# One-pass norms around an early mean, layer 3 two pairs behind layer 2, and the first pair by tiles, in a fused four-layer kernel

## The chip, the cores and the metric

The kernel runs on one core of a Trainium2 chip. The time is that of one execution on the device in microseconds, taken as the median over runs. Five engines work side by side, each on its own queue of instructions in a fixed order: TensorE (PE in the profile, with PEld for its weight loads), VectorE (DVE), ScalarE (ACT), GpSimd (POOL) and SyncE (SP, which issues DMAs here). An engine whose next instruction has to wait holds up everything queued behind it.

## The reference

The input x has the shape (T=4, B=8, 512, 512). Four layers follow one another, each of the form x = x + f(norm(x)). The first is an attention-like block with spiking neurons, the second a 13x13 blur of each channel, the third a quantised 3x3 convolution over the eight channels, the fourth a plain 3x3 convolution over them. In the code these are layer 0 to layer 3.

```python
def _gn(v, G=4, eps=1e-5):                      # group norm
    B_, C_, H_, W_ = v.shape
    g = v.reshape(B_, G, C_ // G, H_, W_)
    m = jnp.mean(g, axis=(2, 3, 4), keepdims=True)
    s = jnp.var(g, axis=(2, 3, 4), keepdims=True)
    return ((g - m) / jnp.sqrt(s + eps)).reshape(v.shape)

x = x + _L0_conv_ref(_gn(x), ...)
x = x + _L1_conv_ref(_gn(x), w1)                # 13x13, each channel alone
# layer 2: sx = 127 / max|v|, sw = 127 / max|w2|, v = _gn(x)
x = x + conv3x3(round(v * sx), round(w2 * sw)) / (sx * sw) + b2
x = x + conv3x3(_gn(x), w3) + b3                # layer 3
```

What matters for the change: `_gn` needs the mean and the variance over two channels of a whole image (index t) before the next layer may use them. Layer 2 needs in addition the largest normed value over all images, for its scale, so it can't start before layer 1 has ended. Layer 3 needs the norm of its own t alone.

## The kernel before

**Layer 1** (class `Layer1`) goes through four groups of two channels, through both channels of each and through the four t. An image is four PSUM tiles of 16 matmuls in the trace. Each tile is evicted by ACT (L850); DVE takes its statistics (`bn_stats`, L852) and its largest and smallest value (`hi` and `lo`, L858) from the evicted tile. `next_norm` makes the mean `m` and the reciprocal deviation `r` of a finished group of channels; for the last group it runs after the last image (the two last `hi` and `lo` reductions of that image are put into its pauses, L905) and nothing of layer 1 is left to lie beside it.

**The norm itself** is `group_steps` (L164 to L198), a generator whose `yield`s let the caller place other work. `bn_stats` leaves a mean and a sum of squared deviations per row and half. A first sum of the means on DVE (`gsum`, L177) goes through a matmul with a constant matrix (`gps`, L180) that adds over the partitions and divides. With the mean back, DVE takes the squared distances of the rows' means, adds the rows' own variances (L189 to L195), sums again, and a second matmul (again L177 and L180) gives the variance. POOL raises it to the power -1/2 (L197).

**Layers 2 and 3** (`layers23`, from L1037) work on windows of rows. Two windows lie on the two halves of the partitions, two such tiles are a pair, and there are 22 pairs in each of the four t, 88 in all; the last pair of a t has half a tile. For a pair of layer 2: SP loads x (L1096), ACT norms it (`y`, L1113), DVE rounds it to `xq` (L1125), POOL copies two outer phase rows of `xq` (L1129 and L1130: a row of pixels is stored as four phases, and a tap to the left of phase 0 is phase 3 moved by one), PE makes three matmuls a tile, one for each dx (L1146), and DVE adds the result to x and writes it into the ring `x3` (L1153). For the statistics of layer 3's norm, rows of t=0 get their sum from this DVE instruction and their squares from ACT (L1160); from t=1 on every second tile does, the others get `bn_stats` on DVE (L1165).

Layer 3 reads the ring. It needs halo rows of neighbouring windows (`halos`; DMAs on SP in the first t, on POOL later, L1304), edge columns (POOL, L1242), and the band of weights scaled with `r` of its own t (`band_t`, L1218). It makes 24 matmuls in the trace per pair (L1249), ACT evicts them (L1258), SP stores them (L1265).

The order is written out in the loop at the end of `layers23`: step n does layer 2 of pair n, then layer 3 of pair n - 22 - `LAG`; `RING` = 23 + `LAG` pairs fit into the ring. `norm3` is started after the last pair of a t and moved on by `next(norm)` twice a step:

```python
        next(norm, None)
        ...
        if n >= N_PAIRS + LAG:
            t, p = divmod(n - N_PAIRS - LAG, N_PAIRS)
            with tc.issue_after(did):
                behind = (layer3(t, p, *norms[t]),)
        if n < n_all and n % N_PAIRS == N_PAIRS - 1:
            norm = norm3(n // N_PAIRS)
        next(norm, None)
```

A scheduler then fixes the order on each engine from this order, moving cheap instructions up where it expects them to be ready; `tc.issue_after` keeps an instruction behind a given one.

Of the kernel before, what the change touches and what calls it, by code (L numbers as in the profile page):

```python
# [35 lines left out]
F32 = mybir.dt.float32  # L36
# [13 lines left out]
G = 4  # L50
# [21 lines left out]
LAG = 3  # L72
# [9 lines left out]
def windows(k):  # L82

    p, j = divmod(k, 2)
    every = [(a, 4 * p + 2 * j + (a ^ j)) for a in range(2)]
    return [(a, q) for a, q in every if q < W_ALL]

# [42 lines left out]
def network(ctx: ExitStack, tc: tile.TileContext, i: dict, out: bass.AP):  # L130
# [68 lines left out]

    def group_stats(*args, **kwargs):  # L200
        steps = group_steps(*args, **kwargs)
        while True:
            try:
                next(steps)
            except StopIteration as end:
                return end.value
# [29 lines left out]
    late = ctx.enter_context(pool("late", side="right"))  # L236
    st2 = late.tile([P, T, B, W1_N // 2 // N_PS1, 6], F32, name="st2")
# [8 lines left out]
    with ExitStack() as s:  # L246
        ps_1 = s.enter_context(pool("ps_2", space=PSUM))
        layer1 = Layer1(
            s, tc, x1d, x2d, avg, group_steps, r1, mr1, st2, m2, r2, most, w_sum, head, ps_1, pool
        )  # L250
        layer1.group(0)
        for g in range(1, G):
            if g == 1:
                with ExitStack() as behind:
                    for op in layer1.started:
                        behind.enter_context(tc.issue_after(op))
                    norm1(G - 1, ps_1)
                    w23 = weights23(tc, i, late, early["y"], ps_1, ident)
            layer1.group(g)
        layer1.next_norm(G - 1)  # L260
    first.close()
    with ExitStack() as s:
        layers23(
            s, tc, x2d, out, ident, ind, mask2, avg_same, group_steps, m2, r2, most, w23, early, pool
        )
# [544 lines left out]
class Layer1:  # L810
    def __init__(
        self, s, tc, x1d, x2d, avg, group_steps, r1, mr1, st2, m2, r2, most, w_sum, head, ps_1, pool
# [3 lines left out]
            nc=nc, x1d=x1d, x2d=x2d, avg=avg, group_steps=group_steps, r1=r1, mr1=mr1, st2=st2, m2=m2,  # L816
# [56 lines left out]
    def group(self, g):  # L873
# [6 lines left out]
        for b in range(g * PAIR, (g + 1) * PAIR):  # L880
# [4 lines left out]
            for t in range(T):  # L885
                self.image(g, b, t, off)
                if g > 0 and b % PAIR == 0 and t == 0:
                    self.next_norm(g - 1)

    def next_norm(self, g):  # L890
# [3 lines left out]
        steps = self.group_steps(  # L894
            self.st2[:, :, g * PAIR : (g + 1) * PAIR].rearrange(
                "p t b k (h z) -> p t (b k h) z", z=3
            ),
            T, PAIR * n_a * 2, None, self.avg, self.ps_1, f"x2_{g}",
        )

        while True:
            try:
                next(steps)
                if g == G - 1 and self.last_ends:
                    nc.vector.tensor_reduce(*self.last_ends.pop(0))  # L905
                next(steps)
            except StopIteration as end:
                m, r = end.value
                break
# [127 lines left out]
def layers23(  # L1037
    s, tc, x2d, out, ident, ind, mask2, avg_same, group_steps, m2, r2, most, w, early, pool
# [81 lines left out]
    def quantise(t, p):  # L1120
# [8 lines left out]
        nc.gpsimd.tensor_copy(xq[:, :, 0, 1:], xq[:, :, PH, : NV - 1])  # L1129
        nc.gpsimd.tensor_copy(xq[:, :, PH + 1, : NV - 1], xq[:, :, 1, 1:])  # L1130
# [6 lines left out]
    def layer2(t, p):  # L1137
# [5 lines left out]
        for j, k in enumerate(ks):  # L1143
            ps = ps_2.tile([P, D], F32, tag="conv2", name="ps_conv2")
            for dx in range(3):
                mm = nc.tensor.matmul(  # L1146
                    ps[:n_p, :], lhsT=w["band2"][:n_p, j, dx, :n_p],
                    rhs=xq[:, j, dx : dx + PH, :], start=dx == 0, stop=dx == 2,
                )
# [43 lines left out]
    def norm3(t):  # L1193
# [3 lines left out]
        ks = by_sums(t)  # L1197
        ks = slice(ks.start, ks.stop, ks.step)
        total, squares = (w["sums"][t % 2][:, j, ks] for j in range(2))
        nc.vector.tensor_scalar_mul(total, total, 1.0 / D)  # L1200
        for h in range(2):
            nc.vector.tensor_copy(st3[:, ks, 3 * h + 1], total)
        nc.vector.tensor_scalar(total, total, w["m"][:, t : t + 1], None, op0=ALU.subtract)
        nc.vector.tensor_mul(total, total, total)
        nc.vector.scalar_tensor_tensor(
            total, total, -1.0 * D, squares, op0=ALU.mult, op1=ALU.add
        )
        for h in range(2):
            nc.vector.tensor_scalar_mul(st3[:, ks, 3 * h + 2], total, 0.5)
        st3 = st3.rearrange("p k (h z) -> p (k h) z", z=3)  # L1210
        nc.vector.tensor_scalar_add(st3[:, :, 1], st3[:, :, 1], w["b2"])
        m, r = yield from group_steps(
            st3.unsqueeze(1), 1, W2_N * 2, mask2, avg_same, ps_1, f"x3_{t}"
# [63 lines left out]
    for n in range(n_all + N_PAIRS + LAG):  # L1277
# [19 lines left out]
        next(norm, None)  # L1297
        if n_chunk < n <= n_all + 3 and n % n_chunk == 3:
            t, p = divmod(n - 3 - n_chunk, N_PAIRS)
            copies = list(halos(t, p, p + n_chunk))  # L1300
            at_once = -(-len(copies) // (n_chunk - 2))
# [3 lines left out]
        if n >= N_PAIRS + LAG:  # L1305
            t, p = divmod(n - N_PAIRS - LAG, N_PAIRS)
            with tc.issue_after(did):
                behind = (layer3(t, p, *norms[t]),)
        if n < n_all and n % N_PAIRS == N_PAIRS - 1:
            norm = norm3(n // N_PAIRS)  # L1310
        next(norm, None)
# [36 lines left out]
```

## Time and profile before

| what | value |
| --- | --- |
| median of 3 runs | 2902.28 us (2898.83 to 2903.59) |
| profiled execution | 2902.63 us, of which the profile's span is 2900.8 us |
| PE busy | 2818.8 us (97%) |
| DVE busy | 2183.1 us (75%) |
| ACT busy | 549.2 us (19%) |
| POOL busy | 868.8 us (30%) |
| last matmul of layer 1 starts | 2482.89 us |
| first matmul of layer 2 starts | 2495.05 us |
| first matmul of layer 3 starts | 2569.18 us |
| last store issued | 2896.87 us |

The times in the profile count from the start of its span. Rows of a timeline give start, length, engine with line, operation, what is written from what, form, and in brackets the idle time of that engine before it with what ended it. Lengths of DVE and PE rows overlap with the next instruction of the same engine: the distance from start to start is what an instruction costs its engine.

### The profile page before, as it was taken

The page shows a single profiled execution, that of the slowest core. Times are in us where ns is not written, and L with a number is a line of the kernel's source. Part 1 is how long each engine was busy: PE and PEld are TensorE (multiplying, and loading weights), DVE is VectorE, ACT ScalarE, POOL GpSimd, SP SyncE. Part 2 cuts the span into 40 slices and gives each one's busy share as a digit, 9 for nine tenths or more (in the row PEclk, how much of TensorE's full clock was granted, in tenths as well). Part 3 has the DMA queues.
Part 4 walks back from the last instruction along what each step waited for, and adds up shares of the span by engine and source line. Part 5 has one row for each costly group of instructions (what it writes and reads, how often), then busy time and mean ns, then how long its engine had stood idle before and what let it go on. Part 6 is the DMA issues. An engine that isn't in the chain of part 4 may idle for free. (4 is left out here: it accounts for less than half of the span.)

```text
span 2900.8 us, 36559 instructions
## 1 busy us (share of the span) xinstructions
PE 2818.8 (97%) x12868; PEld 1302.5 (45%) x12868; DVE 2183.1 (75%) x3888; ACT 549.2 (19%) x851; POOL 868.8 (30%) x1920
## 2 busy tenths in 40 slices
PE   7999999999999999999999999999999999689999
PEld 3444555545555545455555555445333333223334
DVE  6897788788779878878877886886665665888870
ACT  2200100011010001001000000110111121677774
POOL 2242243333234323333422343332311111232220
PEclk9899999999999999999999999999999999999999
DMA  8433222223222232222222122212877788699975
GB/s 209 115 89 76 59 67 67 74 74 74 59 67 67 77 76 68 59 67 67 75 67 51 45 59 52 52 45 75 221 203 207 209 219 224 157 201 234 224 191 148
DMA packets 326127, 324.01 MB, mean 112 GB/s; under 512 B 21519, under 2 KB 240439, under 8 KB 325831
## 3 DMA queue, kind: packets, MB, share of 16 engines
q1 hardware_dynamic: 263024, 239.48, 34.1%
q0 software_dynamic: 19776, 56.14, 6.0%
q10 hardware_dynamic: 43143, 26.05, 3.1%
q8 instruction: 101, 1.65, 0.3%
q14 instruction: 83, 0.68, 0.1%
HBM read 212.44 MB, written 103.65 MB: 109 GB/s over the span
## 5 line engine op out<-in xcount | busy, mean ns | idle before, releaser
L524 PE MATMUL ps_in<-w_v,xn 128*128 128x512 f32 x1024 | 459.1, 599 | 5.4 <-DVE w_v L359 5.4
L524 PE MATMUL ps_in<-w_kq,xn 128*128 128x512 f32 x1024 | 449.8, 592 | 0.0
L843 PE MATMUL ps_conv<-x,bt 112*64 112x512 f32 x2048 | 445.2, 592 | 0.1
L524 PE MATMUL ps_in<-xn,w_kq 128*128 128x512 f32 x1024 | 444.9, 592 | 0.0
L560 PE MATMUL ps_b<-toep,vtok 128*64 128x512 bf16 x3072 | 367.1, 383 | 0.4 <-DVE v_o L575 0.4
L475 ACT ACTIVATE h_q<-v_q,c_half 128x512 f32<-128x512 f32 x96 | 69.1, 721 | 1473.6 <-DVE v_q L471 893.9
L500 POOL TENSOR_TENSOR h_v<-h_v,c_v 128x512 f32<-128x512 f32 x96 | 121.8, 1269 | 728.0 <-DVE h_v L499 700.1
L587 PE MATMUL ps_out<-wp,so 128*128 128x512 f32 x1024 | 308.7, 444 | 0.0
L609 POOL COPY x1s<-x1s 128x2 f32<-128x2 f32 (+1 forms) x1024 | 226.6, 275 | 273.0 <-DVE x1s L598 273.0
L524 PEld LDWEIGHTS ps_in<-xn,w_kq 128*128 128x128 f32 x1024 | 194.3, 190 | 232.5 <-issue 220.4
L524 PEld LDWEIGHTS ps_in<-w_kq,xn 128*128 128x128 f32 x1024 | 194.3, 190 | 220.7 <-issue 206.2
L524 PEld LDWEIGHTS ps_in<-w_v,xn 128*128 128x128 f32 x1024 | 191.4, 191 | 222.9 <-issue 212.1
L843 PEld LDWEIGHTS ps_conv<-x,bt 112*64 112x64 f32 x2048 | 146.5, 135 | 288.0 <-issue 286.0
L560 PEld LDWEIGHTS <-vtok 128*64 128x64 bf16 x3072 | 176.1, 111 | 155.1 <-issue 5.6
L1249 PE MATMUL ps_conv<-x,band_t 64*64 64x512 f32 x2040 | 242.7, 595 | 0.0
L587 PEld LDWEIGHTS ps_out<-wp,so 128*128 128x128 f32 x1024 | 192.6, 188 | 94.0 <-issue 57.8
L1153 DVE SCALAR_TENSOR_TENSOR x<-ps_conv,inv,x 128x512 f32<-128x512 f32 (+1 forms) x172 | 186.1, 1169 | 46.9 <-PE ps_conv L1146 46.7
L598 DVE SCALAR_TENSOR_TENSOR x1s<-v_p,xr 128x256 f32<-128x256 f32 x256 | 187.6, 773 | 14.6 <-DMA x<-x1s 3.8
L865 POOL DMA_DIRECT2D x<-xo x128 | 71.4, 564 | 330.6 <-ACT xo L850 316.3
L850 ACT ACTIVATE xo<-ps_conv,off 128x512 f32<-128x512 f32 x128 | 87.6, 687 | 430.6 <-PE ps_conv L843 307.4
L500 POOL TENSOR_TENSOR h_k<-h_k,c_k 128x512 f32<-128x512 f32 x96 | 122.0, 1270 | 138.4 <-DVE h_k L499 138.4
L1146 PE MATMUL ps_conv<-xq,band 128*128 128x512 bf16 (+1 forms) x516 | 131.5, 391 | 31.3 <-POOL xq L1129 31.3
(193 smaller groups left out, 3113.8 us busy)
## 6 DMA issues: line engine op xcount, KB each, us to landing
x<-x SPq DMA_DIRECT2D x64, 917.0 KB
x<-x SPq DMA_DIRECT2D x168, 256.0 KB
x<-x1s POOLq DMA_DIRECT2D x128, 262.0 KB, 2.7
xq<-in_x SPq DMA_DIRECT2D x128, 256.0 KB
xr<-in_x SPq DMA_DIRECT2D x128, 256.0 KB
out<-o SPq DMA_DIRECT2D x164, 192.0 KB
xs<-in_x SPq DMA_DIRECT2D x112, 256.0 KB
x<-xo ACTq DMA_DIRECT2D x128, 128.0 KB
```

Of the source, the lines that this page charges most:

```text
L500: nc.gpsimd.tensor_add(h, h, c_twice[n])
L524: mm = nc.tensor.matmul(ps, lhsT=lhsT, rhs=rhs, start=k == 0, stop=k == NC - 1)
L560: nc.tensor.matmul(pb[two * DH : (two + 1) * DH, :], lhsT=v[:, c, h * DH : (h + 1) * DH], rhs=toep[z][:, h, u : u + N], start=c == 0 and z ...
L587: nc.tensor.matmul(ps, lhsT=so[:, k, c * P : (c + 1) * P], rhs=wpT[z][:, k, :], start=k == 0 and z == 0, stop=k == NC - 1 and z == 1,)
L598: nc.vector.scalar_tensor_tensor(own, v.rearrange("p (g v) -> p g v", g=PH)[:, two, :], 1.0, by_phase[:, two, :], op0=ALU.is_ge, op1=ALU.add,)
L609: nc.gpsimd.tensor_copy(x1[:, f, u : u + n], x1[:, fm, um - n + 1 : um + 1][:, ::-1])
L843: mm = nc.tensor.matmul(ps[q * M1 : (q + 1) * M1, :], lhsT=bt[:, z, :], rhs=xt[:, w0 : w0 + N_PS1, z : z + NV], start=z == 0, stop=z == SH ...
L850: nc.scalar.activation(xo[:, a, :], ps, AF.Identity, bias=off[:, t : t + 1])
L865: engine.dma_start(bass.AP(dst.tensor, dst.offset + (q * n_half * W1_OUT * B + b) * D + f * NV, [[B * D, W1_OUT], [W1_OUT * B * D, n_half] ...
L1146: mm = nc.tensor.matmul(ps[:n_p, :], lhsT=w["band2"][:n_p, j, dx, :n_p], rhs=xq[:, j, dx : dx + PH, :], start=dx == 0, stop=dx == 2,)
L1153: done["DVE"] = nc.vector.scalar_tensor_tensor(own.rearrange("p (v g) -> p g v", g=PH), by_phase(ps[:n_p, :]), w["inv"][:n_p], by_phase(x[ ...
L1249: mm = nc.tensor.matmul(ps[j][b * HALF : (b + 1) * HALF, :], lhsT=band[half, b, dx, :], rhs=x3[half, s0 + j, dx : dx + D], start=dx == 0, ...
```

## The change

Three things are changed. The norms ahead of layers 2 and 3 no longer end in two sums with a matmul each. A mean of the part that is done early (`centre`) is taken while the layer before still runs: the first channel of the last group ahead of layer 2, the first 17 pairs of a t ahead of layer 3. Distances and squared distances of the rows' means from this centre are summed for the rows that are there (`moments_before`), and the last rows are added in the end (`end_steps`), where one matmul brings both sums; the mean is put right by the centre and the variance by the square of the mean distance. Layer 3 follows two pairs behind the 22 instead of three, and the ring has 25 pairs instead of 26; the halo copies of a half t are spread over fewer steps. In the first pair of layer 2, whose ACT and DVE steps go tile by tile already, POOL's phase rows go tile by tile too, and every pair's matmuls take the middle dx, which needs no phase row, first.

The core of the diff (the passing of the new functions through constructors is left out):

```diff
-LAG = 3
+EARLY = 17
+LAG = 2
 RING = 23 + LAG
...
+    def centre(stats, share, mask, weights, psum, name):
+        gs = [P, stats.shape[1]]
+        part_sum = late_small.tile(gs, F32, tag="csum", name=f"csum_{name}")
+        src = stats[:, :, :, 1]
+        if mask is not None:
+            buf = late_small.tile([P, *stats.shape[1:3]], F32, tag="cbuf", name=f"cbuf_{name}")
+            nc.vector.tensor_mul(buf, src, mask.unsqueeze(1))
+            src = buf
+        nc.vector.tensor_reduce(part_sum, src, AX.X, ALU.add)
+        yield
+        ps = psum.tile(gs, F32, tag="misc", name=f"cps_{name}")
+        nc.tensor.matmul(ps, lhsT=weights, rhs=part_sum, start=True, stop=True)
+        c = late_small.tile(gs, F32, tag="centre", name=f"centre_{name}")
+        nc.vector.tensor_scalar_mul(c, ps, 1.0 / share)
+        return c
+
+    def moments(v, stats, c, mask, n_each=D // 2):
+        shape = list(stats.shape[:3])
+        d, e = v[:, 0], v[:, 1]
+        nc.vector.tensor_sub(d, stats[:, :, :, 1], c.unsqueeze(2).to_broadcast(shape))
+        if mask is not None:
+            nc.vector.tensor_mul(d, d, mask.unsqueeze(1))
+        nc.vector.tensor_mul(e, d, d)
+        nc.vector.scalar_tensor_tensor(
+            e, stats[:, :, :, 2], 1.0 / n_each, e, op0=ALU.mult, op1=ALU.add
+        )
+        if mask is not None:
+            nc.vector.tensor_mul(e, e, mask.unsqueeze(1))
+
+    def moments_before(stats, n_last, c, mask, name):
+        n_groups, n = stats.shape[1:3]
+        v = late_small.tile([P, 2, n_groups, n], F32, tag="mom", name=f"mom_{name}")
+        moments(v, stats, c, mask)
+        last = late_small.tile([P, 2, n_groups, n_last + 1], F32, tag="last", name=f"last_{name}")
+        nc.vector.tensor_reduce(last[:, :, :, n_last], v, AX.X, ALU.add)
+        return last
+
+    def end_steps(stats, last, c, mask, weights, psum, name):
+        n_groups, n = stats.shape[1:3]
+        moments(last[:, :, :, :n], stats, c, mask)
+        part_sum = late_small.tile([P, 2, n_groups], F32, tag="esum", name=f"esum_{name}")
+        yield nc.vector.tensor_reduce(part_sum, last, AX.X, ALU.add).ins
+        ps = psum.tile([P, 2, n_groups], F32, tag="misc", name=f"eps_{name}")
+        nc.tensor.matmul(ps, lhsT=weights, rhs=part_sum, start=True, stop=True)
+        yield
+        got = late_small.tile([P, 2, n_groups], F32, tag="got", name=f"got_{name}")
+        nc.vector.tensor_copy(got, ps)
...
+        nc.vector.tensor_mul(m, got[:, 0, :], got[:, 0, :])
+        op = nc.vector.scalar_tensor_tensor(
+            r, got[:, 1, :], EPS, m, op0=ALU.add, op1=ALU.subtract
+        )
+        nc.gpsimd.tensor_tensor(r, r, neg_half[:, :n_groups], op=ALU.pow)
+        nc.vector.tensor_add(m, got[:, 0, :], c)
+        return m, r, op.ins
...
# Layer1.group
                 self.image(g, b, t, off)
                 if g > 0 and b % PAIR == 0 and t == 0:
                     self.next_norm(g - 1)
+                if (b, t) == (B - 1, 0):
+                    self.before_last()
...
+    def before_last(self):
+        centre, moments_before, _ = self.end
+        done = self.of_channels((G - 1) * PAIR, B - 1)
+        share = (PAIR - 1) / PAIR
+        self.centre = results(centre(done, share, None, self.avg, self.ps_1, "x2"))
+        self.last = moments_before(done, done.shape[2] // (PAIR - 1), self.centre, None, "x2")
+
+    def last_norm(self):
...
+        with tc.issue_after(next(steps)):
+            nc.vector.tensor_reduce(*self.last_ends.pop(0))
+        next(steps)
+        m, r, op = results(steps)
+        with tc.issue_after(op):
+            nc.vector.tensor_reduce(*self.last_ends.pop(0))
+        return m, r
...
# quantise
-        nc.gpsimd.tensor_copy(xq[:, :, 0, 1:], xq[:, :, PH, : NV - 1])
-        nc.gpsimd.tensor_copy(xq[:, :, PH + 1, : NV - 1], xq[:, :, 1, 1:])
+        for j in tiles_apart(t, p, n):
+            nc.gpsimd.tensor_copy(xq[:, j, 0, 1:], xq[:, j, PH, : NV - 1])
+            nc.gpsimd.tensor_copy(xq[:, j, PH + 1, : NV - 1], xq[:, j, 1, 1:])
# layer2
-            for dx in range(3):
+            for dx in (1, 0, 2):
...
# norm3: means() and part() are the former code, on rows k0 to k1
+        k1, k2 = 2 * EARLY, W2_N - 1
+        means(0, k1)
+        first = part(0, k1).unsqueeze(1)
+        share = (4 * EARLY * W_STEP + 1) / N
+        c = yield from centre(first, share, mask2[:, : 2 * k1], avg_same, ps_1, name)
+        yield
+        means(k1, k2)
+        part(k1, k2)
+        before = st3[:, :k2, :].rearrange("p k (h z) -> p (k h) z", z=3).unsqueeze(1)
+        last = moments_before(before, 2, c, mask2[:, : 2 * k2], name)
+        yield
+        m, r, _ = yield from end_steps(
+            part(k2, W2_N).unsqueeze(1), last, c, mask2[:, 2 * k2 :], avg_same, ps_1, name
+        )
...
# the loop
-        next(norm, None)
+        p = n % N_PAIRS
+        if p < LAG:
+            next(norm, None)
...
-            at_once = -(-len(copies) // (n_chunk - 2))
+            at_once = -(-len(copies) // (n_chunk - 4))
...
-        if n < n_all and n % N_PAIRS == N_PAIRS - 1:
+        if n < n_all and p == EARLY:
             norm = norm3(n // N_PAIRS)
-        next(norm, None)
+        if p < LAG or p in (EARLY, EARLY + 1, N_PAIRS - 2, N_PAIRS - 1):
+            next(norm, None)
```

## The prediction

> **What bounds the kernel now.** I read the page first. Its row of forty slices has PE at 9 everywhere but in the first slice (a 7, which the change doesn't touch) and in slices 35 and 36 (a 6 and an 8), so only two places can give or take much: the passage from layer 1 into layer 2, and the stretch after it in which layer 2 runs alone. Next the table of stages of those parts (columns: length, then busy time of PE, PEld, DVE, ACT, POOL, granted clock, DMA share):
>
> ```profile
> 2497.00:2550.00 53.00, 30.91 (x125) 12.20 (x124) 52.85 (x103) 51.51 (x100) 14.63 (x40) 0.99 0.79 164
> 2550.00:2561.00 11.00, 3.81 (x14) 2.03 (x14) 8.12 (x29) 4.10 (x7) 2.66 (x6) 0.64 1.08 222
> ...
> 2583.00:2640.00 57.00, 57.00 (x416) 18.20 (x408) 44.57 (x70) 42.02 (x69) 15.12 (x44) 1.00 0.95 255
> 2640.00:2664.00 24.00, 23.05 (x159) 8.21 (x161) 22.49 (x50) 15.73 (x25) 7.47 (x17) 1.00 0.94 188
> ...
> 2839.00:2894.00 55.00, 55.00 (x503) 28.11 (x496) 0.15 (x1) 29.25 (x43) 1.15 (x9) 1.00 0.54 159
> ```
>
> The fill (image t=0 of layer 2) is bound by DVE: 52.85 of 53 us busy, 2.59 us a pair. Then comes a hole of 10 us around the norm of t=0. From 2569 on PE is full: a pair of both layers takes 4.14 us (1.40 us of layer 2, 2.74 of layer 3), and DVE needs 3.2 of these, so it has 0.9 us to spare per pair. What DVE does is free there unless PE waits for it, and the PE waits after 2610 us name one thing: the gps matmul for gsum, 2.2 us over five times.
>
> The timeline of the first passage:
>
> ```profile
> 2484.23 0.69 DVE L852 BATCH_NORM_STATS2 st<-xo 128x6 f32<-128x512 f32 x1 [1.57 <-ACT xo L850]
> ...
> 2485.43 0.23 DVE L177 TENSOR_REDUCE gsum_x<-st 128x4 f32<-128x64 f32 x1
> ...
> 2487.33 0.21 DVE L177 TENSOR_REDUCE gsum_x<-gbuf_x 128x4 f32<-128x64 f32 x1
> ...
> 2488.33 1.02 POOL L197 TENSOR_TENSOR grstd_x<-grstd_x,neg_half 128x4 f32<-128x4 f32 x1 [1.61 <-DVE grstd_x L196]
> 2489.39 0.17 DVE L911 COPY r<-grstd_x 128x4 f32<-128x4 f32 x1 [1.21 <-POOL grstd_x L197]
> ...
> 2492.56 3.78 ACT L1113 ACTIVATE y<-x,mr_own,r_own 128x512 f32<-128x512 f32 x4 [8.36 <-DVE mr_own L1070]
> ...
> 2495.05 4.42 PE L1146 MATMUL ps_conv<-xq,band 128*128 128x512 bf16 x12 [3.25 <-POOL xq L1129]
> ```
>
> The reader sees two round trips DVE-PE-DVE (two gsum), then POOL's power, then the first pair, whose matmul waits for POOL's phase row of both tiles.
>
> [...] a 128x1 op takes 0.15 us, and a dependent one starts 0.19 us after the one before. [...] Here the first twelve bf16 matmuls start 0.43 us apart, later ones 0.22.
>
> **The change part by part.**
>
> (1) Norm ahead of layer 2. Removed are one round trip and four 64-column ops; what stays behind the last BN is sub, mul, add, reduce on 32 to 72 columns. At 0.22 us each from 2484.95: esum starts 2485.6, its result is back 0.73 us later (as gsum's), behind the last hi reduction; copy, square and variance at 0.19 end at 2486.9; POOL's power starts 0.16 later and takes 1.02; DVE meanwhile has the last lo (0.59) and seven short ops at 0.1, done at 2488.1. The r copy comes at 2488.15, not 2489.39: **-1.24**. Its early mean puts one matmul into layer 1, where PE is full: the gps matmuls there put the next convolution off by 0.40: **+0.40**. The early DVE ops (six, under 1.5 us) lie in DVE's idle 5.7 us before each image's bands.
>
> (2) First pair. From y at Y, the first xq ends Y+1.28. The middle tap needs only this: PE at Y+1.34 in place of Y+2.49, x at Y+2.8 in place of Y+3.97. But xq of pair 1 stands ahead of x on DVE until Y+3.3, so x gains less; followed to pair 1's x (Y+5.87 against Y+6.84): **-0.95**. Two more POOL copies (0.3 each) end before their taps.
>
> (3) Norm of t=0, where DVE is the bound:
>
> ```profile
> 2550.55 0.19 DVE L1200 TENSOR_SCALAR sums<-sums 128x42 f32<-128x42 f32 x1
> ...
> 2554.74 0.24 DVE L177 TENSOR_REDUCE gsum_x<-gbuf_x 128x1 f32<-128x86 f32 x1
> ...
> 2558.79 0.62 DVE L1218 SCALAR_TENSOR_TENSOR band_t<-band,grstd_x,eye 128x384 f32<-128x384 f32 x1 [0.69 <-POOL grstd_x L197]
> ```
>
> The early sums (twelve ops on 34 or 68 columns at pairs 17 and 18) go straight onto DVE: +1.5. The run ahead of pair 21's x grows from 0.96 to 1.75: +0.8. Behind its BN now stand twelve ops (to esum's end, 1.8 where it was 1.1 to gsum's), one trip of 0.68, three short ops and POOL's 0.7, so band starts 4.34 us after BN's start instead of 5.50: -1.16. Together **+1.15**. PE's extra matmul is free here.
>
> (4) Layer 3 two pairs behind. PE begins layer 3 after pair 24 instead of 25. In the trace pair 24's matmuls end 2567.0 and layer 3 begins 2569.18; 2.2 us come earlier, the 1.4 us of pair 25 are still to do, and middle taps first give 0.5: **-1.3**. The ring of 25 is as tight as that of 26 was: x of pair n overwrites what layer 3 read one step before. Output DMAs start a pair earlier, their rate is unchanged. Then the bubble (0.64, pair 28 at 2580.90), from POOL's timeline:
>
> ```profile
> 2578.34 0.19 POOL L1242 COPY x<-zero 128x4 f32<-128x4 f32 x1 [2.66 <-DMA x<-x]
> 2578.89 1.55 POOL L1304 DMA_DIRECT2D x<-x  x2 [0.36 <-issue]
> 2580.44 0.41 POOL L1129 COPY xq<-xq 128x254 bf16<-128x254 bf16 x1
> ```
>
> An edge copy waits for a halo DMA issued at 2564.78, and xq queues behind it. With one layer-3 pair more ahead of that matmul, PE gets there at about 2581.0 on the old clock against 2580.2 for POOL: **-0.64**, with 0.8 us of slack.
>
> (5) Norms of t=1 and t=2, where PE is full:
>
> ```profile
> 2642.82 0.21 DVE L1200 TENSOR_SCALAR sums<-sums 128x21 f32<-128x21 f32 x1
> ...
> 2644.85 1.20 DVE L1153 SCALAR_TENSOR_TENSOR x<-ps_conv,inv,x 64x512 f32<-64x512 f32 x1
> ...
> 2648.02 0.24 DVE L177 TENSOR_REDUCE gsum_x<-gbuf_x 128x1 f32<-128x86 f32 x1
> ```
>
> PE reaches gps at 2647.6 and waits until 2648.32. What ended late is DVE: eight ops (2.03 us) ahead of the last x, three (0.97) behind it. Now there are fifteen ahead of it, five of them full rows of 84 columns in a dependent chain (0.30 each) and a two-row reduce: uncontended 2.53 against the 1.48 of t=3, **1.05 more**; behind it seven dependent ones at 0.19, 0.45 more. The queue holds esum ahead of pair 44's x, so nothing lets it by. The wait at eps becomes 0.70 + 1.5 = 2.2 us. Saved are the second gps (0.31) and its wait (0.25); the early matmul costs 0.40 in a full PE. The early DVE ops cost nothing: DVE's 0.9 us a pair takes their 1.7 within two pairs. **+1.34 each, 2.7.** What is late next, band and const, has over 1 us: PE does two layer-3 pairs and one and a half of layer 2 between eps and const.
>
> (6) Norm of t=3. The same DVE run, gap 0.37 to about 1.9 (+1.5), second gps saved (0.31), early matmul 0.40: **+1.6**. Layer 3's pairs 20 and 21 (4.1 us) cover the rest of the chain (2.5).
>
> Sum: 0.40 - 1.24 - 0.95 + 1.15 - 1.3 - 0.64 + 2.7 + 1.6 = **+1.7 us**. The profiled execution took 2902.63 us (span 2900.8), so 2904.35; it lies 0.35 above the median 2902.28, hence 2904.0.
>
> Bounds of what the trace doesn't show: the fifteen ops may fit in DVE's idle time (no added wait) or be stretched by POOL as three of eight were (up to twice); half clock after the norm may take 0.5 from step 4 or nothing.
>
> **Rivals.**
> A. The norms' ends pay: DVE takes the added ops in its slack and eps waits no longer than gps did (0.70, 0.70, 0.37). For it: DVE is idle 0.9 us before most pairs. Against: at 2642 to 2654 the timeline shows it with no idle time. 4.5 us less than the sum: 2899.5. With step 3's additions hidden too, 2897 or below.
> B. Slower: VectorE's queue at the three norms. [...] fifteen take 4 us and seven 1.9, 1.5 us more at each norm, all of it PE's: 2908.5. It decides from about 4 us between sums and the last x.
> C. Slower: the third halo copy (issued 2564.78, awaited until 2578.34) lands later than 13.5 us; DMA is at 1.00 from 2561 to 2583. Beyond 0.8 us PE pays one for one: 5 us late is 2908.
> D. That early sums are put off to the end is excluded by the issue order.
>
> **How the numbers follow.** The forecast 0.62, A 0.15, B 0.15, C 0.08. A measurement tells 0.2%, 5.8 us, from no change: faster by more needs nearly all of A and its extra (0.08); slower by more takes half of B and C and a little of the forecast (0.18); within it 0.74. The range 2897.5 to 2909.5 takes in A and B.
>
> **What would show it.** Right: first y about 1 us earlier after layer 1's last matmul, layer 3 starting directly behind pair 24, eps waits of about 2 us at t=1 to 3, no bubble at pair 28. Wrong: eps waits under 1 us (A), over 3 (B), or POOL's edge wait reaching PE (C).

## The result, and the profile after

Over eleven runs each, the changed kernel took 2909.07 us in the median (2907.2 to 2913.4), the kernel before 2901.04 (2898.8 to 2903.6). The ratio is 1.0029, with a 95% interval of 1.0019 to 1.0038: **slower by 0.3%**. The forecast was +1.7 us, 2904.0, with a range up to 2909.5. The median lies inside that range by 0.4 us, but the medians differ by 8.0 us: a difference under 5.8 us had been given a chance of 0.74, slower by more than that 0.18. The profiled execution spans 2907.2 us, 6.4 more than that of before (2900.8), which took 1.6 us more than the median of its kernel.

The table of stages of the changed kernel, columns as before (length, busy time of PE, PEld, DVE, ACT, POOL, granted clock, DMA share, and last the DMA rate in GB/s):

```profile
2492.00:2547.00 55.00, 37.39 (x127) 11.08 (x128) 53.86 (x112) 52.45 (x99) 16.08 (x44) 0.98 0.69 160
2547.00:2560.00 13.00, 5.41 (x19) 1.80 (x16) 11.09 (x42) 6.22 (x11) 3.38 (x9) 0.72 0.98 212
...
2641.00:2664.00 23.00, 20.46 (x128) 7.06 (x130) 19.51 (x50) 12.53 (x20) 5.44 (x14) 0.93 0.94 205
2842.00:2900.00 58.00, 58.00 (x527) 29.78 (x520) 0.59 (x3) 30.19 (x45) 3.83 (x22) 1.00 0.56 158
```

The fill is still DVE's (53.86 of 55 us busy) and the tail still PE's (58.00 of 58). New is the third row: around the norm of t=1 PE now lacks 2.5 us of its 23, where it lacked 0.95 of 24, and the granted clock of that stretch is 0.93, where it was 1.00.

The passage from layer 1 into layer 2, as a timeline (start, length, engine, what it does, and in brackets the idle time before it):

```profile
2483.47 0.69 DVE L924 BATCH_NORM_STATS2 st<-xo 128x6 f32<-128x512 f32 x1 [1.56 <-ACT xo L922]
...
2484.88 0.23 DVE L256 TENSOR_REDUCE esum_x<-last_x 128x8 f32<-128x72 f32 x1
...
2486.26 1.02 POOL L268 TENSOR_TENSOR erstd_x<-erstd_x,neg_half 128x4 f32<-128x4 f32 x1 [0.31 <-DVE erstd_x L265]
...
2490.63 2.65 ACT L1203 ACTIVATE y<-x,mr_own,r_own 128x512 f32<-128x512 f32 x3 [7.19 <-DVE mr_own L1160]
...
2492.05 1.44 PE L1238 MATMUL ps_conv<-xq,band 128*128 128x512 bf16 x3 [2.18 <-DVE xq L1215]
```

From the last bn_stats of layer 1 to the first y it is 7.16 us (8.33 before), from y to the first matmul of layer 2 1.42 (2.49 before). The first matmul now waits for one tile's xq on DVE (2.18 us), no longer for POOL (3.25). This part went as forecast.

PE behind the norm of t=0:

```profile
2558.48 0.38 PE L1339 MATMUL ps_const<-scaled,sum 64*64 64x1 f32 x4 [2.02 <-DVE scaled L1334]
2559.73 0.61 PE L1238 MATMUL ps_conv<-xq,band 128*128 128x512 bf16 x1 [0.86 <-DVE xq L1215]
2560.76 0.61 PE L1238 MATMUL ps_conv<-xq,band 128*128 128x512 bf16 x1 [0.43 <-DVE x L1245]
2562.84 4.07 PE L1238 MATMUL ps_conv<-xq,band 128*128 128x512 bf16 x10 [1.46 <-DVE xq L1215]
2566.84 1.52 PE L1361 MATMUL ps_conv<-x,band_t 64*64 64x512 f32 x12
```

Two pairs of layer 2 are twelve matmuls, and here they run as one, one and ten. A middle tap needs no POOL copy, so the scheduler could expect it to be ready early, and it moved three of them up: first tile and second tile of pair 23, and the first tile of pair 24. The third waits for the rounding of pair 24 (the idle 1.46 us), and the outer taps of pair 23 stand behind it. In the trace of before these two pairs run six and six.

The norm of t=1, DVE and PE, and then PE of the kernel before at the same place:

```profile
2643.63 0.14 DVE L1295 TENSOR_SCALAR sums<-sums 128x4 f32<-128x4 f32 x1
...
2644.77 0.58 DVE L1309 TENSOR_SCALAR st<-st,b 128x16 f32<-128x16 f32 x1
...
2647.31 1.14 DVE L1245 SCALAR_TENSOR_TENSOR x<-ps_conv,inv,x 64x512 f32<-64x512 f32 x1
...
2649.94 0.37 DVE L232 TENSOR_TENSOR last_x<-st,centre_x 128x2 f32<-128x2 f32 x1
...
2651.27 0.16 DVE L256 TENSOR_REDUCE esum_x<-last_x 128x2 f32<-128x6 f32 x1
```

```profile
2651.49 0.39 PE L258 MATMUL eps_x<-esum_x,avg_same 128*128 128x2 f32 x2 [2.54 <-DVE esum_x L256]
2651.80 4.44 PE L1361 MATMUL ps_conv<-x,band_t 64*64 64x512 f32 x24
2656.17 1.47 PE L1238 MATMUL ps_conv<-xq,band 128*128 128x512 bf16 x6
```

```profile
2648.32 0.38 PE L180 MATMUL gps_x<-gsum_x,avg_same 128*128 128x1 f32 x2 [0.70 <-DVE gsum_x L177]
2648.64 2.81 PE L1249 MATMUL ps_conv<-x,band_t 64*64 64x512 f32 x24
2651.37 1.47 PE L1146 MATMUL ps_conv<-xq,band 128*128 128x512 bf16 x6
```

DVE's run ahead of the last x is 3.68 us long (2.03 before), and PE stands 2.54 us for eps (0.70 for gps before). Then comes what the forecast had not seen: the layer-3 pair behind eps takes 4.37 us to the next pair instead of 2.74. The table of stages for three short windows (the wait, the pair behind it, the next pair) says why in its column of the granted clock, third from the right:

```profile
2648.20:2651.40 3.20, 0.75 (x4) 0.14 (x2) 2.96 (x11) 0.67 (x2) 1.30 (x3) 1.00 0.88 150
2651.50:2655.00 3.50, 3.50 (x18) 1.33 (x22) 3.43 (x9) 1.43 (x3) 0.00 (x0) 0.53 1.09 225
2655.20:2657.50 2.30, 2.30 (x18) 0.65 (x10) 0.58 (x2) 1.53 (x3) 1.91 (x6) 1.00 0.88 107
```

PE is busy all through the second window (3.50 of 3.50 us), at about half its clock (0.53).

Where the 6.4 us of the profiled executions are, in us; the parts add up to 6.35:

| stretch | forecast | measured |
| --- | --- | --- |
| up to the end of layer 1 | +0.40 | -0.76 |
| norm ahead of layer 2, to the first y | -1.24 | -1.17 |
| first pair, from y to DVE's pace in the fill | -0.95 | -0.57 |
| norm of t=0, to the first x behind it | +1.15 | +1.45 |
| from there until pair 25 of layer 2 (the first is pair 0) and the first pair of layer 3 are done | -1.3 | +0.12 |
| bubble at pair 28 | -0.64 | -0.70 |
| norm of t=1 | +1.34 | +3.07 |
| norm of t=2 | +1.34 | +3.40 |
| norm of t=3 | +1.6 | +1.51 |

The first row says nothing: the end of layer 1 differs by over 3 us between the profiled executions of kernels that are equal up to there.

### The profile page after: what moved, and what is told of

Its sections match the earlier page's. It is cut to its first block, busy times and chain, and to the rows that moved or that the text cites. A ratio compares the mean times of both kernels' runs of the same rounds, so it can differ in the third digit from the quotient of the medians.

```text
span 2907.2 us, 36645 instructions
## 1 busy us (share of the span) xinstructions
PE 2827.5 (97%) x12868; PEld 1301.2 (45%) x12868; DVE 2196.5 (76%) x3975; ACT 550.5 (19%) x851; POOL 866.8 (30%) x1922
## 3 DMA queue, kind: packets, MB, share of 16 engines
q8 instruction: 101, 1.65, 0.2%
## 5 line engine op out<-in xcount | busy, mean ns | idle before, releaser
L1238 PE MATMUL ps_conv<-xq,band 128*128 128x512 bf16 (+1 forms) x516 | 137.5, 391 | 26.5 <-DVE xq L1215 23.1
```

What stands on the lines that cost most here:

```text
L1238: mm = nc.tensor.matmul(ps[:n_p, :], lhsT=w["band2"][:n_p, j, dx, :n_p], rhs=xq[:, j, dx : dx + PH, :], start=dx == 1, stop=dx == 2,)
```

## The experiments

The theory: the change's losses are two, the DVE run at the norms of t=1 to 3 (with the clock behind it) and the order of taps behind the norm of t=0. Rivals stand in each expectation. One yardstick serves all: PE is full from t=1 on (in the kernel before 66.00 of 66.00 us from 2664 on), so the time from the start of one image's 19th pair of layer 3 to that of the next image's holds one norm and nothing else that changes.

| kernel (times in us) | over the norm of t=1 | over that of t=2 | wait at eps or first gps, t=1, 2, 3 | pair behind it, t=1, 2 |
| --- | --- | --- | --- | --- |
| before | 92.10 | 91.99 | 0.70, 0.60, 0.37 | 2.74, 2.74 |
| after | 95.17 | 95.38 | 2.54, 2.69, 1.96 | 4.37, 4.44 |
| plain taps | 96.63 | 93.69 | 2.52, 2.69, 1.95 | 5.33, 2.74 |
| early moments | 92.21 | 92.29 | 1.22, 1.29, 0.97 | 2.74, 2.74 |
| PE kept busy | 94.14 | 94.26 | filled, filled, 1.95 | 2.74, 2.74 |
| old norm ahead of layer 3 | 97.13 | 96.66 | 0.70, 0.63, 0.32 | see below |

**Plain taps**

```diff
-            for dx in (1, 0, 2):
+            for i, dx in enumerate((1, 0, 2) if (t, p) == (0, 0) else (0, 1, 2)):
...
-                    rhs=xq[:, j, dx : dx + PH, :], start=dx == 1, stop=dx == 2,
+                    rhs=xq[:, j, dx : dx + PH, :], start=i == 0, stop=i == 2,
```

> The changed kernel with the taps of layer 2 in their old order (left, middle, right) in every pair but the first. In the changed kernel's trace, after the norm of t=0, PE runs one middle tap at 2559.73 and one at 2560.76 and then stands until 2562.84 for the quantised pair 24: the issue order put three middle taps (pair 23 both tiles, pair 24 first tile) ahead of pair 23's outer taps. Theory (middle taps first cost the gain of the shorter lag): without it pair 23's first x starts on DVE at about 2562.8 in place of 2564.3, layer 3 starts 0.8 us earlier after const (7.5 us in place of 8.36), and the time is about 0.8 us below the changed kernel: 2908.3, ratio to before 1.0025. Rival (DVE alone sets the pace of these two pairs, the order of taps is hidden): layer 3 starts 8.3 us after const as now, 2909. Neither touches the norms: eps waits stay 2.5, 2.7 and 2.0 us.

Measured: 2907.93 us, ratio 1.0018 (1.0011 to 1.0026). Its PE timeline behind the norm of t=0:

```profile
2561.07 0.38 PE L1339 MATMUL ps_const<-scaled,sum 64*64 64x1 f32 x4 [2.02 <-DVE scaled L1334]
2562.86 2.72 PE L1238 MATMUL ps_conv<-xq,band 128*128 128x512 bf16 x6 [1.41 <-POOL xq L1220]
2565.94 1.79 PE L1238 MATMUL ps_conv<-xq,band 128*128 128x512 bf16 x6 [0.36 <-POOL xq L1220]
2567.66 2.81 PE L1361 MATMUL ps_conv<-x,band_t 64*64 64x512 f32 x24
```

The pairs run six and six again, and layer 3 starts 6.59 us after const in place of 8.36. That is 1.8 us, not 0.8, and not all of it is the order: PE's clock came up within pair 24 here (matmuls 0.22 us apart), 5.6 us after const, and in the changed kernel only at that pair's end (0.43), 7.9 us after const. A cleaner comparison is that of "early moments" with "both edits" below, which differ in the order of taps alone and whose clocks come up 7.2 and 7.1 us after const: layer 3 starts 7.98 and 7.36 us after it. So the order costs some 0.6 us there, up to 1.0 if the changed kernel is set against "both edits", and the rival of a hidden order falls in the traces. In time plain taps bring 1 to 3 us; the two intervals overlap.

The row of this kernel in the table above is the cleanest sight of the clock: one kernel, waits of 2.52 and 2.69 us, and the *shorter* one cost the clock. The two images differ by 2.94 us. Behind the longer wait, at t=2:

```profile
2749.10 0.38 PE L258 MATMUL eps_x<-esum_x,avg_same 128*128 128x2 f32 x2 [2.69 <-DVE esum_x L256]
2749.41 2.81 PE L1361 MATMUL ps_conv<-x,band_t 64*64 64x512 f32 x24
```

**Early moments**

```diff
         c = yield from centre(first, share, mask2[:, : 2 * k1], avg_same, ps_1, name)
+        last = moments_before(first, 2 * (W2_N - k1), c, mask2[:, : 2 * k1], name)
         yield
         means(k1, k2)
-        part(k1, k2)
-        before = st3[:, :k2, :].rearrange("p k (h z) -> p (k h) z", z=3).unsqueeze(1)
-        last = moments_before(before, 2, c, mask2[:, : 2 * k2], name)
         yield
         m, r, _ = yield from end_steps(
-            part(k2, W2_N).unsqueeze(1), last, c, mask2[:, 2 * k2 :], avg_same, ps_1, name
+            part(k1, W2_N).unsqueeze(1), last, c, mask2[:, 2 * k1 :], avg_same, ps_1, name
         )
```

> The changed kernel with layer 3's moments split elsewhere: those of the first 34 rows are taken at pair 18, right behind the early mean, where DVE has 0.9 us to spare per pair; only the last 9 rows (18 columns) are left for the ops behind the last x. Ahead of the last x stand 8 ops again in place of 15, behind it 7 as now. Theory (the wait at eps is the DVE run ahead of the last x, and PE's clock drops when that wait is long enough): eps waits 1.2, 1.2 and 1.0 us in place of 2.5, 2.7 and 2.0, no half clock after them, so 3.0 us each at t=1 and t=2 and 0.9 at t=3: 2902.2, ratio to before 1.0004. Rival (the seven ops behind the last x and the quantise ahead of them set the wait): eps waits stay over 2 us and the time over 2907. Second rival (the early ops on PE-full pairs are not free): eps waits fall but the pairs 18 to 20 lengthen, 2905 or more.

Measured: 2904.10 us, ratio 1.0005 (0.9996 to 1.0013), 0.24% below the changed kernel's ratio, against 0.25% expected. DVE and PE at t=1:

```profile
2642.84 0.14 DVE L1295 TENSOR_SCALAR sums<-sums 128x4 f32<-128x4 f32 x1
...
2645.06 1.16 DVE L1245 SCALAR_TENSOR_TENSOR x<-ps_conv,inv,x 64x512 f32<-64x512 f32 x1
...
2649.11 0.19 DVE L256 TENSOR_REDUCE esum_x<-last_x 128x2 f32<-128x38 f32 x1
```

```profile
2649.36 0.38 PE L258 MATMUL eps_x<-esum_x,avg_same 128*128 128x2 f32 x2 [1.22 <-DVE esum_x L256]
2649.67 2.81 PE L1359 MATMUL ps_conv<-x,band_t 64*64 64x512 f32 x24
```

The run ahead of the last x is 2.22 us in place of 3.68, the wait 1.22, and the clock stays up. Both images are back within 0.3 us of before: the moved ops cost nothing at pair 18. The rival that the seven ops behind the last x set the wait falls; they are still there. What the one-pass norm brings at t=1 and 2 is then seen too: nothing (+0.1 and +0.3 us). The second round trip was hidden there all along but for 0.6 us.

**PE kept busy**

```diff
+        if n in (2 * N_PAIRS, 3 * N_PAIRS):
+            ps = ps_1.tile([P, D], F32, tag="misc", name="ps_busy")
+            wide = w["band2"].rearrange("p j x c -> p (j x c)")
+            for _ in range(10):
+                nc.tensor.matmul(ps, lhsT=wide[:, :P], rhs=wide[:, :D], start=True, stop=True)
         if p < LAG:
             next(norm, None)
```

> The changed kernel with ten matmuls of 128x512 in bf16 put on PE just ahead of the eps matmul at t=1 and t=2, into a PSUM tile that nobody reads (2.2 us of PE at full clock, inside a wait of 2.5 us). Nothing else is removed, DVE's run is the same. Theory (1.65 us of the loss at each of these norms is PE's clock, which drops after the wait): eps starts when it did, the layer-3 pair behind it takes 2.74 us in place of 4.4, and the time falls by about 3.3 us to 2905.8, ratio 1.0016, although PE got more to do. Rival (the slow matmuls behind eps come from something else at that place[...]): the pair stays at 4.4 us, the time at 2909 or, with the wait overrun, up to 2910.

Measured: 2909.30 us, ratio 1.0023 (1.0013 to 1.0033): no gain in time. The PE timeline at t=1, and then at t=3, where nothing was added:

```profile
2650.28 2.32 PE L1414 MATMUL ps_busy<-band 128*128 128x512 bf16 x10
2652.53 1.07 PE L1361 MATMUL ps_conv<-x,band_t 64*64 64x512 f32 x2
2653.53 0.38 PE L258 MATMUL eps_x<-esum_x,avg_same 128*128 128x2 f32 x2
2653.84 2.80 PE L1361 MATMUL ps_conv<-x,band_t 64*64 64x512 f32 x22
...
2839.39 0.38 PE L258 MATMUL eps_x<-esum_x,avg_same 128*128 128x2 f32 x2 [1.95 <-DVE esum_x L256]
2839.70 5.84 PE L1361 MATMUL ps_conv<-x,band_t 64*64 64x512 f32 x28
```

The theory held: with PE busy the layer-3 pair behind eps is back at 2.74 us, from 4.37 and 4.44, and each of the two images is 1.0 and 1.1 us shorter although PE did 2.2 us more. The expected size did not: at t=1 eps came 0.56 us later than without the extra matmuls (the scheduler put two of layer 3 ahead of it), which leaves 1.1 of 1.65. And at t=3 a wait of 1.95 us, which had cost no clock in the changed kernel, cost 1.7 us in this one. Together 0.5 us, too little to be measured.

**How long a wait costs the clock.** The probe, on the changed kernel's last image; in the first version the copy stands behind the eviction of its tile, in the second ahead of it:

```diff
+    def probe(n_ops):
+        nc.vector.tensor_copy(late, last_ps[0][:, :1])
+        for _ in range(n_ops):
+            nc.vector.tensor_scalar_mul(late, late, 0.5)
+        ps = ps_1.tile([P, 1], F32, tag="misc", name="ps_probe")
+        return nc.tensor.matmul(ps, lhsT=avg_same, rhs=late, start=True, stop=True).ins
...
                 behind = (layer3(t, p0, *norms[t]),)
+            if t == T - 1 and p0 in PROBE:
+                did = probe(PROBE[p0])
```

> The changed kernel with a measured wait put on PE behind each of 20 layer-3 pairs of the last image, where nothing else runs on DVE: a copy of one column from the pair's PSUM tile, 2 to 14 dependent one-column ops, and a one-column matmul that needs them, ahead of the next pair. Waits of about 0.9, 1.3, 1.7, 2.0, 2.4, 2.8 and 3.2 us, each about three times. Theory (PE's clock drops after a wait by chance, by how the wait falls on a fixed grid of time; so far 2.54, 2.69, 2.6 and 1.95 us dropped it, 1.96, 1.96, 2.69 did not, 1.4 or less never): no drop up to 1.4 us, some from 1.7 on, most or all at 3.2. A drop shows as a pair of 4.4 us or so in place of 2.74. Rival (what drops the clock is something else at the norms, not the wait): no slow pair here at any wait. Time in all about 45 us more plus 1.6 for each drop.

> The probe again with shorter waits: the one-column copy now stands ahead of the eviction of its tile (it had waited for ScalarE, which made every wait 1.2 us longer than meant), and 2 to 8 dependent ops follow. Waits of about 0.9 to 2.1 us in steps of 0.19, each about three times. The first probe had no untouched pair above 2.1 us and one of two touched at 2.06. Theory (a window of fixed length must hold enough idle time, so the chance grows with the wait): no slow pair below some 1.4 us, a part of the pairs slow, often only from their middle on, between 1.5 and 2.1. Rival (a sharp bound on the length of the wait, about 2 us): all pairs at 2.74 us up to 1.9. In both the waits of 1.3 to 1.4 us at the norms with early moments stay on the safe side.

Measured (one run each, 3028.9 and 2955.5 us with the waits in them). The waits of the first probe came out at 2.06 to 4.33 us, longer than meant, and its time at 120 us over the changed kernel's, not the 75 or so that 45 us and 1.6 for each of 19 slow pairs make. Two waits from its PE timeline, then one from the second's:

```profile
2907.75 0.35 PE L1396 MATMUL ps_probe<-late_rhs,avg_same 128*128 128x1 f32 x2 [2.06 <-DVE late_rhs L1394]
2908.03 2.81 PE L1362 MATMUL ps_conv<-x,band_t 64*64 64x512 f32 x24
2914.03 0.56 PE L1396 MATMUL ps_probe<-late_rhs,avg_same 128*128 128x1 f32 x2 [3.19 <-DVE late_rhs L1394]
2914.51 5.40 PE L1362 MATMUL ps_conv<-x,band_t 64*64 64x512 f32 x24
```

```profile
2894.05 0.35 PE L1396 MATMUL ps_probe<-late_rhs,avg_same 128*128 128x1 f32 x2 [1.91 <-DVE late_rhs L1394]
2894.33 4.50 PE L1364 MATMUL ps_conv<-x,band_t 64*64 64x512 f32 x24
```

A pair that keeps its clock reads 2.81 us, one that loses it at once 5.4, one that loses it on the way, or gets it back, in between. All waits of the two probes and of eps and gps at the norms (t=1 to 3) of the kernels here, without the last wait of each probe, behind which only a quarter of a pair stands:

| wait, us | slow pairs in the probes | at the norms |
| --- | --- | --- |
| up to 1.15 | 0 of 8 | 0 |
| 1.22 to 1.34 | 1 of 3 | 0 of 6 |
| 1.52 to 1.72 | 1 of 5 | none |
| 1.90 to 2.06 | 3 of 5 | 1 of 5 |
| 2.44 to 2.83 | 7 of 7 | 7 of 8 |
| 3.18 to 4.33 | 10 of 10 | none |

The rival that something else at the norms slows PE falls, and so does a sharp bound on the length of the wait. So does "no slow pair below some 1.4 us": one wait of 1.30 us cost the clock. The share of slow pairs rises with the wait from about 1.3 us on and is near one at 2.5. A slow pair takes 1.5 to 2.6 us longer.

The grid of time that these expectations speak of is in the traces. In each of the eleven executions all changes of the granted clock lie on one grid of 3.41 us (to within 6 ns, from the first change to the last), so the time can be cut into its windows. The kernel with plain taps, around the waits of t=1 and t=2 (length, PE busy, granted clock, DMA share, GB/s):

```profile
2648.57:2651.99 3.42, 1.15 (x5) 1.00 0.74 147
2651.99:2655.40 3.41, 3.11 (x14) 0.50 1.07 223
...
2744.15:2747.56 3.41, 2.20 (x13) 1.00 0.79 108
2747.56:2750.97 3.41, 1.87 (x18) 1.00 1.03 275
```

The shorter wait left PE idle for 2.27 us of one window, and the next two windows had half clock. The longer one was cut by the grid into windows with 1.21 and 1.54 us idle, and the clock stayed. In the same way the wait of 1.95 us at t=3 of "PE kept busy" lay in one window, that of 1.96 us in the changed kernel in two (1.36 and 0.60 us). Counted over all eleven traces, from the first matmul of layer 3 to the last, for the windows with full clock: none of 1015 with up to 1.29 us idle was followed by half clock, three of 14 with 1.30 to 1.71 us, and all 31 with 1.90 us or more. Two things stay open: the three, and why in the fill of t=0, where PE has other matmuls, windows with 1.96 us idle kept the clock.

**The old norm ahead of layer 3**

```diff
-        k1, k2 = 2 * EARLY, W2_N - 1
...
-        m, r, _ = yield from end_steps(
-            part(k2, W2_N).unsqueeze(1), last, c, mask2[:, 2 * k2 :], avg_same, ps_1, name
+        m, r = yield from group_steps(
+            st3.unsqueeze(1), 1, W2_N * 2, mask2, avg_same, ps_1, f"x3_{t}"
         )
...
-        if n < n_all and p == EARLY:
+        if n < n_all and p == N_PAIRS - 1:
             norm = norm3(n // N_PAIRS)
```

> The changed kernel with the old two-pass norm ahead of layer 3 at all four images (its steps from pair 21 on, two a pair), all else as changed: the one-pass norm ahead of layer 2, the first pair tile by tile, middle taps first, layer 3 two pairs behind. Theory (all of the loss is the new norm ahead of layer 3): the first y 2.2 us earlier after layer 1's last matmul, which the DVE-bound fill passes on, no bubble at pair 28 (0.7), nothing else: 2898.2, ratio 0.999, so 10.9 us below the changed kernel. gps waits 0.7, 0.7 and 0.4 us again. Rival (the shorter lag costs too: ring of 25, more halo copies a pair, const one pair before layer 3): layer 3 starts later after const or POOL's edge copies wait on a halo landing again, 2901 to 2903.

Measured: 2909.15 us, ratio 1.0027 (1.0016 to 1.0038). **The expectation failed by 11 us.** DVE and PE at t=1:

```profile
2654.66 0.13 DVE L205 TENSOR_SCALAR grstd_x<-gps_x 128x1 f32<-128x1 f32 x1
...
2656.16 2.11 DVE L1245 SCALAR_TENSOR_TENSOR x<-ps_conv,inv,x 128x512 f32<-128x512 f32 x2 [0.77 <-PE ps_conv L1238]
...
2659.30 0.63 DVE L1310 SCALAR_TENSOR_TENSOR band_t<-band,grstd_x,eye 128x384 f32<-128x384 f32 x1
```

```profile
2660.07 0.61 PE L1341 MATMUL ps_conv<-x,band_t 64*64 64x512 f32 x1 [3.30 <-DVE scaled L1314]
```

The gps waits are short again, as expected. But the band of the new t, made one pair later than in the one-pass norm, stands in DVE's queue behind the x of one more pair, and layer 3, now only two pairs behind, reaches it first: PE stands 3.3 us (up to 2660.07) and runs slow after (4.72 us from there to the next matmul of layer 2, const's matmuls among them, where a pair at full clock takes 2.74), and the same again at t=2. In the kernel before, with a lag of three, PE has no such wait (after 2610 us only those at gps, 0.7 us at the longest). So the shorter lag and the one-pass norm are not two edits: the second is what the first needs at t=1 and 2, and taking one away alone doesn't show its price.

**Both edits, the boundary alone, and a mixed version.** The first has the edits "plain taps" and "early moments" as shown. The second is the kernel before with the new norm ahead of layer 2 and the new first pair only; against the changed kernel it has the edits "plain taps" and "old norm", and:

```diff
-LAG = 2
+LAG = 3
...
-            at_once = -(-len(copies) // (n_chunk - 4))
+            at_once = -(-len(copies) // (n_chunk - 2))
```

The third is the first with the norm of t=0 in two passes:

```diff
+        m, r = yield from (two_pass if t == 0 else one_pass)(t)
...
-        if n < n_all and p == EARLY:
+        if n == N_PAIRS - 1 or N_PAIRS < n < n_all and p == EARLY:
             norm = norm3(n // N_PAIRS)
```

> Both edits together: the moments of the first 34 rows taken at pair 18 (only 18 columns left for the ops behind the last x), and the old order of taps in every pair but the first. Theory (two separate losses, each seen alone): eps waits 1.3, 1.4 and 1.0 us and no half clock behind them, as with the early moments alone; layer 3 of t=0 starts 6.3 us after const in place of 8.0. Against before: first layer-2 matmul 2.25 us earlier, const 2.45 later from there, 1.7 less up to the end of pair 25, bubble of 0.7 gone, 0.5 more over the three later norms: 2901, ratio 0.9995. Rival (the tap order matters only where the long run of DVE ops stands): no gain over early moments alone, 2904.

> The kernel before with two parts of the change alone: the one-pass norm ahead of layer 2, and the first pair tile by tile with its middle tap first. Two-pass norms ahead of layer 3, layer 3 three pairs behind, old order of taps elsewhere. Theory (what is gained ahead of the first x of layer 2 is kept, since DVE sets the pace from there): first y 7.9 us and first layer-2 matmul 9.3 us after layer 1's last matmul (9.1 and 11.6 before), const 64.7 us after that matmul as before, everything later unchanged, bubble at pair 28 included: 2900.2, ratio 0.9993. Rival (the early mean inside layer 1 costs PE as much as the end saves): 2902.5.

> As both edits together, and the norm of t=0 alone in its old two-pass form, its steps from pair 21 on. There DVE is the bound, and the trace of the changed kernel shows its early sums at pairs 17 and 18 as 1.8 us and its longer run ahead of the last x as 0.7 us, against 1.1 us saved behind it. Theory: const comes 64.7 us after the first layer-2 matmul in place of 67.0, of which the later band (one pair later in the order) gives back about 0.7: 2899.5, ratio 0.999, the fastest so far. Rival (a two-pass norm cannot feed a layer 3 that is two pairs behind: the old norm at all images waited 3.3 us for its band at t=1): layer 3 starts 8 us or more after const and nothing is gained over both edits, 2901 or more.

| kernel | median, us | ratio to before (interval) | first layer-2 matmul to const | const to layer 3 |
| --- | --- | --- | --- | --- |
| both edits | 2902.18 | 0.9997 (0.9989 to 1.0005) | 66.88 | 7.36 |
| boundary alone | 2899.51 | 0.9989 (0.9981 to 0.9998) | 65.27 | 9.64 |
| two passes at t=0 | 2899.07 | 0.9989 (0.9982 to 0.9995) | 65.24 | 6.58 |

In before, after and the old norm of the experiment above these stretches are 64.49, 66.43 and 64.66, and 9.64, 8.36 and 8.73 us. Both edits come near the 2901 us expected of them, with eps waits of 1.32, 1.25 and 0.95 us; layer 3 starts later behind const than expected (7.36, not 6.3), and since the interval overlaps that of the early moments alone, the times don't exclude the rival, only the traces speak against it (7.36 and 7.98, as above). The boundary alone gives the gain that was expected of it: the early mean inside layer 1 costs less than the end saves. Two passes at t=0 bring const 1.6 us earlier, and there the lag of two works with the old norm too (6.58): the rival falls. That 6.58 lies 0.8 below 7.36 is the clock and not the edit: half clock ended 5.6 us after const here, 7.1 us with both edits. Layer 3 of an earlier t does not run there; whether that is why the band was not late was not followed up. Both versions beat the kernel before and the changed one; between them the runs can't tell. The starts of DVE's x at t=0, counted from the first layer-2 matmul, show where one pass loses:

| tile | before | after | two passes at t=0 |
| --- | --- | --- | --- |
| 2nd | 2.76 | 3.12 | 3.12 |
| 34th | 44.25 | 44.75 | 44.82 |
| 37th (past the early sums) | 48.46 | 50.75 | 49.08 |
| 43rd, the last | 57.06 | 60.15 | 57.73 |
| 1st of the next t, past the norm | 65.58 | 67.53 | 66.34 |

## Why the prediction came out as it did

**Right.** The passage into layer 2 (step 1): 1.17 us against 1.24. The end chain of the norm of t=0: from the last x to the first behind it 1.14 us shorter, against 1.16. The bubble: 0.70 against 0.64, though the boundary alone, with the old lag, shrinks it to 0.22 as well, so it wasn't the lag's doing alone. The norm of t=3 (step 6): 1.51 against 1.6. That the loss would sit at the norms and begin with DVE's run was right as well.

**Luck.** The range reached up to 2909.5 for the sake of rival B, whose own number, 2908.5, is close to the median. But B's sign, waits over 3 us, did not come, and most of what filled the range, 3.3 us, is a cost that neither the sum nor a rival had. With a forecast of +1.7 us and 8.0 us measured, that the median lies inside is luck.

**Mis-sized.** Step 2: pair 1's x gained 0.71 from y and 0.14 of that went in the next pairs; 0.95 was forecast. Step 3: the early sums at t=0 cost 1.79, not 1.5, and the run ahead of the last x 0.80 as forecast. Step 5's run on DVE: the "fifteen ops" ahead of the last x took 3.68 us, 1.65 more than before in place of "1.05 more", and the seven behind it about 0.75 more in place of 0.45. The prediction priced them by their times at t=3, and the trace shows single ones at 0.58, 0.40 and 0.37 us while POOL copies lie beside them; the same three take 0.23, 0.16 and 0.16 us at t=3, where none does. (Of the ops that took longer at t=1 than at t=3 in the kernel before, the two copies of sums, 0.49 us against 0.27, ended as POOL's copies began, beside an issue of a DMA by POOL; beside the copies themselves stood the next two, at 0.42 and 0.30 us against 0.24 and 0.18.) This is the direction of rival B, at a quarter to two fifths of its 1.5 us: the wait at eps grew to 2.5 and 2.7 us, not 2.2. B's own 4 and 1.9 us for the two runs of ops were the author's estimate. That POOL is the cause was not tested.

**Wrong: "What is late next, band and const, has over 1 us".** That sentence of step 5 closed the account of t=1 and t=2 with the wait. Band and const were in time; what was late next was PE's own clock, 1.63 and 1.70 us. The prediction knew of half clock, but only as a remnant of the 10 us hole at t=0 and in the first pair of layer 2. (There not all twelve matmuls start 0.43 us apart: in the trace of before the first nine do, at 0.38 to 0.43, and the last three follow at 0.22 to 0.24.) That a wait of 2.2 us leaves the clock whole was the author's assumption, which was not shown: in the kernel before PE's longest wait after 2610 us was 0.7 us. The runs speak against it. From the first matmul of layer 3 to the last, 1.90 us or more of idle time in one window of the 3.41 us grid was followed by half clock in all 31 cases, and by their length waits of 2.44 to 2.83 us cost the clock in 14 of 15 cases, those of 1.2 to 2.1 us in six of 24.

**Wrong: step 4's "middle taps first give 0.5".** They cost some 0.6 to 1.0. The lag's own gain, 0.8 of the forecast's 1.3, is there: with both edits, where the clock comes up at the same point as before, that stretch is 0.9 us shorter than before (with plain taps 1.65, of which 0.8 is a clock that came up earlier). In the changed kernel the order of PE's queue eats it. The step looked at one pair's dependences; the scheduler looked at all.

The profile has 4.7 us more than the forecast's +1.7. The clock is 3.3 of it, the order of taps 1.4 (the 0.5 that it did not give and what it cost), the longer waits at t=1 and 2 are 0.9, steps 2 and 3 together 0.7. Going the other way are 1.2 at the end of layer 1 (which no experiment explains, see above) and 0.5 for the early matmul and the second gps at t=1 and 2.

## What to carry to other kernels

Work that is taken out of the end of a serial chain lands somewhere in the same queue: count what then stands ahead of the chain's *last input*, because that delays the end just as well, and cut the work so that only the last rows are left (here 15 ops to 8, worth 0.24% of the whole kernel). By these runs, price a wait on TensorE of over some 1.3 us with a chance of half clock behind it (six of 24 between 1.2 and 2.1 us), and one of 2.5 us (14 of 15) at its own length plus 1.7 (one window of 3.41 us at half clock), at times 2.6. Do not read a difference of 1 or 2 us behind such a wait as the work of an edit before the clock of both kernels there has been compared. An edit that makes an instruction ready earlier lets a scheduler move it, so read the queue around every place where the instruction occurs, not only where it was meant to help.

## What the runs showed of the hardware

In all eleven traces the granted clock changes on a grid of 3.41 us, and from the first matmul of layer 3 to the last the spells of half clock last one window or two. One wait of PE of 1.30 us was followed by half clock, and one of 2.69 us (plain taps, t=2) left the clock whole. The time that PE stands within one window tells more than the length of the wait: 1.90 us and more cost the clock in all 31 cases there, up to 1.29 us in none of 1015, and in between in three of 14. The loss may come late, at the next edge of the grid: up to 1.5 us after PE had resumed.
